# Two layers of causal attention on one core: row maxima taken two heads at a time, and a mask as products

## The chip, the core and the metric

The kernel runs on one core of a Trainium2 chip. Its time is the device time of one launch in microseconds (us); three runs before the change gave 3539.60, 3553.49 and 3558.32, a median of 3553.49. The engines are called as the profile calls them: PE is TensorE's matrix product, PEld its weight load, DVE is VectorE, ACT is ScalarE, POOL is GpSimd, and SP issues most transfers. Products are written to PSUM, which has eight banks of 512 float32 columns on 128 partitions.

## The reference, cut to what matters

```python
def _L0_ffn_ref(...):                       # layer 0, on xn = layernorm(x), as x below
    ...                                     # layernorm, Wqkv, rope
    scores = jnp.einsum('bqhd,bkhd->bhqk', q, k) / math.sqrt(hd)
    scores = jnp.where(causal, scores, -1000000000.0)
    probs = jax.nn.softmax(scores, axis=-1)
    attn = jnp.einsum('bhqk,bkhd->bqhd', probs, v).reshape(Bb, Tt, d) @ Wproj
    x = x + attn
    ...                                     # 8 experts, top 2, capacity 1024

def _L1_attn_ref(x, Wq, Wk, Wv, Wo):        # layer 1
    ...
    scores = (einsum(q_r, k_r) + einsum(q_i, k_i)) / jnp.sqrt(jnp.float32(hd))
    scores = jnp.where(causal[None, None], scores, -jnp.inf)
    probs = jax.nn.softmax(scores, axis=-1)
    ...                                     # times v_r, v_i, then Wo

x = L0_attn_x                               # 2 x 2048 x 256, 16 heads
x = x + _L0_attn_ref(xn) * silu(_L0_ffn_ref(xn))   # a linear attention beside the softmax attention
x = x + _L1_attn_ref(xn) * silu(_L1_ffn_ref(xn))   # xn is the layernorm of the new x
```

Both layers have a causal softmax attention over 2048 tokens, two batches and sixteen heads. A softmax needs the largest score of each row first.

## The kernel before

The work has three stages: layer 0's attention with a linear attention beside it, the experts, and layer 1's attention with its gates. Both attentions are made by `run_attention` (L513). Heads go in eight groups of four (two batches, four groups); the four heads of a group stand in four row groups of 32 partitions, so that four score products can run in the array side by side.

Each score is computed twice. **Pass A** (`pass_a`, L530) has queries on the partitions: for query tile `t` (128 queries) and key block `k` (up to 512 keys) the product of head `j` goes to a bank of its own (L535), and DVE takes the largest of each row. Off the diagonal it is one `tensor_reduce` (L546). On the diagonal (`k == t // 4`) the mask has to be added: `tensor_tensor_reduce` (L542) adds a table `causal` and takes the maximum; on the chip it is two instructions, the masked maximum and the read of its accumulator. When all tiles of a query block `c` (256 queries) are done, `subtract` brings the maxima to the other pass: in layer 0 they are added to the queries (L774 on), in layer 1 they become three bfloat16 rows that a product adds (`less_maximum`, L1485). **Pass B** (`pass_b`, L554) has keys on the partitions: the products of L561, on the diagonal a mask that is added by four bfloat16 products of 256 columns (`hide`, L500 to L504: `ident_h` times `mask_h`), then the exponential on ACT (L573). The weights times the values are products in column tiling (L803 in layer 0, L1516 in layer 1); in layer 1 POOL adds up the keys' weights (L1497 to L1502).

One step `u` of the loop handles one (t, k) of pass A for four heads and one key pair of pass B, one query block behind. Within it, two half units: heads `i` and `i + 1` do pass A while heads `i + 2` and `i + 3` do pass B, the four products alternating; then the pairs swap.

The order of the instructions isn't that of the loop. Every piece of work is a step with an engine, a price and the buffers that it reads and writes (`Plan.step`, L147). `Plan.run` (L273) searches, with a beam over random handicaps, for an order of all steps of a layer, and `places` (L181) gives each buffer the place of its kind that has been free for longest. PSUM banks are the kind `s`: eight places, each a tile of its own (`banks`, L446). Strand S is the main stream of PE, A the maxima, B the exponentials, V the sums of values; prep, sub, end, lin, mix and gate are other strands, and some of them may only hold a limited number of banks. The prices of the steps are the kernel's own (`t_row`, `t_dve`, `t_act`, L434 to L443).

Of the kernel before, what the change touches and what calls it, by code (L numbers as in the profile page):

```python
# [30 lines left out]
C_CAUSAL = C_ID + P  # L31
C_TRI = C_CAUSAL + 512
C_AFTER = C_TRI + P
# [8 lines left out]
def _constants():  # L42

    c = np.zeros((P, C_ALL), np.float32)
    r = np.arange(P)
    c[:, C_ID : C_ID + P] = np.eye(P)
    c[:, C_CAUSAL + 384 : C_CAUSAL + 512] = np.where(r[None] <= r[:, None], 0.0, FAR)
    c[:, C_TRI : C_TRI + P] = r[:, None] <= r[None]
    c[:, C_AFTER : C_AFTER + P] = np.where(r[:, None] > r[None], FAR, 0.0)
    c[:, C_BLOCK : C_BLOCK + P] = r[:, None] // 16 == r[None] // 16  # L50
    c[:, C_H8 : C_H8 + 8] = r[:, None] // 16 == np.arange(8)[None]
    c[:, C_H4 : C_H4 + 4] = r[:, None] // 32 == np.arange(4)[None]
    c[:, C_EREV : C_EREV + E] = E - np.arange(E)
    c[:, C_EIDX : C_EIDX + E] = np.arange(E)
    return c
# [15 lines left out]
class Buf:  # L71

    def __init__(self, kind):
        self.kind, self.n, self.uses, self.t = kind, None, 0, None

# [8 lines left out]
class State:  # L86


    def __init__(self, plan):
# [6 lines left out]
        self.guest = [None] * len(plan.bufs)  # L96
        self.since = {k: [0.0] * len(x) for k, x in plan.kinds.items()}
        self.free, self.groups = {}, [0.0] * 4
# [12 lines left out]
class Plan:  # L111
# [14 lines left out]


    GAP = 0.1
    MODE = 0.2
# [51 lines left out]
    def places(self, st, strand, s, t):  # L181

        take = []
        for b in s.bufs:
            if st.slot[b.n] is None:
                if b.kind == "s" and strand != "S" and st.held.get(strand, 0) >= self.QUOTA.get(strand, 1):
                    if sum(st.held.values()) >= self.GUESTS:
                        return None
                taken = [i for x, i in take if x.kind == b.kind]
                at, n = None, None  # L190
                for i, x in enumerate(st.since[b.kind]):
                    if x is not None and (at is None or x < at) and i not in taken:
                        at, n = x, i
# [6 lines left out]
    def advance(self, st, handicaps, until):  # L200
# [3 lines left out]
        while st.todo:  # L204
# [36 lines left out]
            for b, i in take:  # L241
                st.slot[b.n], st.since[b.kind][i] = i, None
                if b.kind == "s" and key[0] != "S":
                    st.guest[b.n] = key[0]
                    st.held[key[0]] = st.held.get(key[0], 0) + 1
# [18 lines left out]
            for b in s.bufs:  # L264
                st.left[b.n] -= 1
                st.until[b.n] = max(st.until[b.n], done)
                if st.left[b.n] == 0:
                    if st.guest[b.n]:
                        st.held[st.guest[b.n]] -= 1
                    st.since[b.kind][st.slot[b.n]] = st.until[b.n]  # L270
        return True

    def run(self):  # L273
# [36 lines left out]
        for s, take in order:  # L310
            for b, i in take:
                b.t = self.kinds[b.kind][i]()
            s.fn()
# [4 lines left out]
def kernel(ctx: ExitStack, tc: tile.TileContext, i: dict, out: bass.AP):  # L318
# [14 lines left out]
    ident = cst[:, C_ID : C_ID + P]  # L333
    causal = cst[:, C_CAUSAL : C_CAUSAL + 512]
    h4 = cst[:, C_H4 : C_H4 + 4]
# [39 lines left out]
    early = ctx.enter_context(ExitStack())  # L375
    w0 = early.enter_context(tc.tile_pool(name="w0", bufs=1))
    prelude = ctx.enter_context(ExitStack())
    pool = prelude.enter_context(tc.tile_pool(name="prelude", bufs=1))
# [20 lines left out]
    nc.sync.dma_start(wgate, rows(i["L0_ffn_Wgate"]))  # L399
    for n, c in enumerate((C_ID, C_AFTER)):  # L400
        m = bank().rearrange("p (q n) -> p q n", q=4)
        for q in range(4):
# [6 lines left out]
            )  # L409
        if n == 0:  # L410
            nc.vector.tensor_copy(ident_h, m)
        else:
            nc.vector.tensor_copy(mask_h, m[:, :, None].to_broadcast([P, 4, 2, P]))
    tp = bank("t")
# [30 lines left out]

    def banks(ps, names):  # L446
        return [lambda n=n: ps.tile([P, 512], F32, tag=n, name=n, bufs=1) for n in names]

# [50 lines left out]

    def hide(out, j):  # L500

        r = slice(32 * j, 32 * j + 32)
        for q in range(4):
            nc.tensor.matmul(out, ident_h[r, q], mask_h[r, q].rearrange("p n k -> p (n k)"), start=False, stop=q == 3)  # L504

# [6 lines left out]

    def run_attention(plan, make, prepare, subtract, sum_keys, finish, last_sum, before=None, others=(), between=False):  # L513

# [14 lines left out]

        def pass_a(g, t, k, j, w, mx, parts):  # L530

            s, r, out = Buf("s"), slice(32 * j, 32 * j + 32), (mx, t, k, j)

            def score():
                nc.tensor.matmul(  # L535
                    s.t[:, :w], g.qt.t[r, t * P : (t + 1) * P], g.kt.t[r, 512 * k : 512 * k + w], start=True, stop=True
                )

            def largest():
                to = mx.t[:, t % 2, j, k : k + 1]  # L540
                if k == t // 4:
                    nc.vector.tensor_tensor_reduce(  # L542
                        s.t[:, :w], s.t[:, :w], causal[:, 512 - w :], 1.0, -3e38, ALU.add, ALU.max, to
                    )
                else:
                    nc.vector.tensor_reduce(to, s.t[:, :w], AX.X, ALU.max)  # L546

            keys = range(4 * k, 4 * k + -(-w // P))
            step = S("S", "PE", t_row(w), score, r=[(g.qt, t), *((g.kt, n) for n in keys)], w=[s], on=j)
            S("A", "DVE", t_dve(w) + (0.19 if k == t // 4 else 0.0), largest, r=[s], w=[out])  # L550
            parts.append(out)
            return step

        def pass_b(g, c, p, j, pt):  # L554
# [11 lines left out]
            def rest():  # L566
                if before:
                    S("S", "PE", 0.25 * t_row(w), before(g, c, j, s, w, not diagonal), r=[s, g.mh[c]], w=[s], on=j)
                if diagonal:
                    S("S", "PE", T_HIDE, lambda: hide(s.t[:, : 2 * P], j), r=[s], w=[s], on=j)  # L570

# [9 lines left out]
        for u in range(at + last_sum + 1):  # L581
# [11 lines left out]
            for i in (0, 2):  # L593


                more = []
                for x in range(2):
                    if a:
                        plan.pace = pass_a(g, t, k, i + x, wa, mx, parts)
                        first = first or plan.pace  # L600
                    if b:
                        step, rest, weigh = pass_b(gb, cb, p, (i + 2 + x) % 4, pt)
                        first = first or step
                        more.append((rest, weigh))
                for rest, _ in more:
                    rest()
# [35 lines left out]
    with ExitStack() as sc:  # L642
# [13 lines left out]
        for vt in vts:  # L656
# [12 lines left out]
            dict(  # L669
                s=banks(ps, [f"s{n}" for n in range(8)]),  # L670
                qt=slots(wk, "qt", 2, [P, T]), kt=slots(wk, "kt", 2, [P, T]),
# [543 lines left out]
    for mpad in mpads1:  # L1215
        nc.gpsimd.memset(mpad, 0.0)
    lts = [w.tile([17, 512], F32, name=f"lt{n}") for n in range(2)]
    for lt in lts:
        nc.gpsimd.memset(lt, 1.0)

# [104 lines left out]
    with ExitStack() as sc:  # L1325
# [4 lines left out]
            dict(  # L1330
                s=banks(ps, [f"s{n}" for n in range(8)]),
                qt=slots(wk, "qt", 2, [P, T]), kt=slots(wk, "kt", 2, [P, T]), vt=slots(wk, "vt", 2, [P, NT, 4, 32]),
# [10 lines left out]
        S = plan.step  # L1343
        stats = norms(w, S)
        turned = {}

# [232 lines left out]
        def gate(b, c):  # L1579

            xt, pa, lt, ln = turned[b], Buf("s"), lts[c % 2], ("lt", c % 2)
            x_in_c = [(xt, c, t) for t in range(4 * c, 4 * c + 4)]
# [48 lines left out]
        others.sort(key=lambda x: x[0])  # L1631
        run_attention(plan, Group1, prepare, subtract, sum_keys, finish, SUM_LAG, less_maximum, others)
        with tc.manual_schedule():
# [29 lines left out]
```

## Time and profile before

| what | value |
|---|---|
| median of three runs | 3553.49 us |
| profiled execution | 3519.21 us, span 3517.3 us, mean granted clock 0.965 |
| PE, PEld busy | 3354.9 us (95%), 2382.7 us (68%) |
| DVE busy | 2160.5 us (61%) |
| ACT, POOL busy | 1680.8 us (48%), 1653.3 us (47%) |
| chain that ended last, by engine | PE 80%, POOL 11%, DVE 3%, waits for issue 2%, ACT 2% |
| layer 0, from 280 to 1130 us | PE 844.4, PEld 631.1, DVE 648.9, ACT 484.4, POOL 261.5 us |
| layer 1, from 2200 to 3400 us | PE 1179.8, PEld 834.3, DVE 820.1, ACT 620.1, POOL 937.9 us |

The page's groups name the line, the engine and operation, the written and read tiles, then the shapes (partitions x elements), the number of instructions, their busy time in us and the mean of one in ns, and last the idle time of the engine just before them with what ended most of it. "32*128" is the tiling of the array in rows and columns: 32*128 are the row-tiled score products, 128*32 the column-tiled products with the values, 128*128 the whole array. The ends of products are modelled by the profiler, so a product's record is longer than the time for which it fills the array; products in other row groups overlap it. Profiled execution and timed runs differ by 34 us, or 1%.

### The profile page before, as it was taken

What the parts mean: (1) busy time and instruction counts of PE and PEld (TensorE: products, weight loads), DVE (VectorE), ACT (ScalarE), POOL (GpSimd) and SP (SyncE); (2) the same over time, 40 slices, a digit from 0 to 9 for tenths busy, and PEclk for the clock granted to TensorE, in tenths of its full rate; (3) what the DMA queues carried; (4) which work ended last, traced back from release to release, by engine and by line L of the source; (5) the groups of instructions that cost most, each with busy time, mean ns of one, the idle gap of its engine ahead of it and who ended that gap; (6) DMA issues with size and microseconds to landing.
All of it is one profiled execution on the core that took longest, in us unless ns stands there. A gap on an engine that the chain in (4) does not pass through costs nothing.

```text
span 3517.3 us, 81236 instructions
## 1 busy us (share of the span) xinstructions
PE 3354.9 (95%) x33814; PEld 2382.7 (68%) x33814; DVE 2160.5 (61%) x5577; ACT 1680.8 (48%) x3341; POOL 1653.3 (47%) x2222
## 2 busy tenths in 40 slices
PE   6999999999999999599999699999999999999998
PEld 4777777777777776466666366666776667777775
DVE  5777777777777776411111366766666657667674
ACT  3565655555556555121111355545455555454544
POOL 4443222333233213300000357989777667877877
PEclk7999999999999999699999899999999999999998
DMA  5000000000000000222221211111000010000000
GB/s 180 2 2 2 8 8 8 19 29 16 8 11 5 14 8 24 84 68 74 78 72 46 89 53 43 33 43 31 21 8 27 31 39 14 22 13 22 11 19 28
DMA packets 88017, 115.38 MB, mean 33 GB/s; under 512 B 9043, under 2 KB 67103, under 8 KB 87650
## 3 DMA queue, kind: packets, MB, share of 16 engines
q1 hardware_dynamic: 81506, 96.32, 8.6%
q0 software_dynamic: 6144, 13.88, 1.3%
q8 instruction: 265, 4.34, 0.5%
q14 instruction: 102, 0.84, 0.1%
HBM read 75.33 MB, written 37.75 MB: 32 GB/s over the span
## 4 chain that ended last, share of the span: by engine, by line
PE 80%; POOL 11%; DVE 3%; issue 2%; ACT 2%; DMA 1%; SPq 0%; POOLq 0%; ACTq 0%; DVEq 0%
PE s L561 15%; PE s L535 14%; PE s L803 7%; PE s L1302 6%; PE s L1308 6%; PE s L1516 5%; PE s L1427 3%; PE s L504 3%; PE s L735 3%; POOL ps L1501 2%; PE s L1485 2%; POOL ps L1502 2%; POOL ps L1497 2%; PE s L359 2%; PE s L1522 2%
## 5 line engine op out<-in xcount | busy, mean ns | idle before, releaser
L573 ACT ACTIVATE pt<-s 128x512 f32<-128x512 f32 (+1 forms) x2304 | 1169.1, 576 | 709.2 <-PE s L561 246.0
L561 PE MATMUL s<-qt,kt 32*128 32x256 f32 (+1 forms) x9216 | 1297.6, 391 | 7.5 <-DVE un L810 3.3
L535 PE MATMUL s<-kt,qt 32*128 32x512 f32 (+3 forms) x5120 | 1269.8, 561 | 5.1 <-ACT pt L573 2.0
L546 DVE TENSOR_REDUCE mx<-s 128x1 f32<-128x512 f32 x1536 | 961.0, 682 | 193.2 <-PE s L535 111.4
L561 PEld LDWEIGHTS s<-qt,kt 32*128 32x128 f32 x9216 | 990.2, 187 | 61.3 <-ACT pt L573 9.8
L535 PEld LDWEIGHTS s<-kt,qt 32*128 32x128 f32 x5120 | 531.5, 187 | 165.0 <-issue 97.0
L542 DVE CUSTOM_DVE_ANT_0 s<-s,cst 128x128 f32<-128x128 f32 (+3 forms) x1024 | 481.3, 514 | 102.0 <-PE s L535 81.8
L1497 POOL TENSOR_TENSOR ps<-pt 128x1024 f32<-128x1024 f32 (+1 forms) x160 | 343.2, 2145 | 150.0 <-ACT pt L573 129.2
L742 POOL TENSOR_TENSOR ra<-raw,rope 128x128 f32<-128x128 f32 x128 | 58.6, 458 | 640.4 <-ACT raw L754 599.9
L1501 POOL TENSOR_TENSOR ps<-ps,pt 128x1024 f32<-128x1024 f32 x128 | 302.4, 2363 | 68.4 <-ACT pt L573 63.8
L1485 PE MATMUL s<-mh,ones_h 3*128 3x512 bf16 (+1 forms) x1152 | 321.9, 370 | 1.1 <-ACT mh L1478 1.1
L1362 POOL DMA_INDIRECT gx<-slots_out,back x64 | 62.8, 982 | 498.0 <-issue 496.4
L1311 DVE TENSOR_TENSOR ye<-s,b 128x256 f32<-128x256 f32 x64 | 27.2, 424 | 410.8 <-PE s L1308 410.8
L803 PE MATMUL s<-pt,vt 128*32 128x256 f32 (+1 forms) x4608 | 274.6, 377 | 0.6 <-ACT raw L754 0.5
L1502 POOL TENSOR_TENSOR ps<-ps,pt 128x1024 f32<-128x1024 f32 (+1 forms) x128 | 269.9, 2109 | 10.0
L1516 PE MATMUL s<-pt,vt 128*32 128x256 f32 (+1 forms) x4608 | 272.3, 375 | 0.7 <-ACT pt L573 0.4
L1303 ACT ACTIVATE hm<-s,b1c 128x512 f32<-128x512 f32 x128 | 87.8, 687 | 360.8 <-PE s L1302 360.8
L1302 PE MATMUL s<-xt,w 128*128 128x512 f32 x512 | 225.0, 598 | 7.1 <-DVE xt L1274 7.0
L1516 PEld LDWEIGHTS s<-pt,vt 128*32 128x32 f32 x4608 | 134.6, 111 | 137.9 <-ACT pt L573 19.7
L1308 PE MATMUL s<-w,hm 128*128 128x256 f32 x1024 | 223.6, 379 | 0.0
L803 PEld LDWEIGHTS s<-pt,vt 128*32 128x32 f32 x4608 | 135.3, 111 | 125.3 <-issue 21.9
L1308 PEld LDWEIGHTS s<-w,hm 128*128 128x128 f32 x1024 | 194.7, 190 | 33.1 <-issue 7.6
(257 smaller groups left out, 4240.6 us busy)
## 6 DMA issues: line engine op xcount, KB each, us to landing
w<-in_L_ffn_W_dram SPq DMA_DIRECT2D x16, 1024.0 KB, 5.6
gl<-g_dram SPq DMA_DIRECT2D x64, 256.0 KB, 2.7
slots_in<-zero SPq DMA_DIRECT2D x8, 1024.0 KB, 10.1
xe<-slots_in SPq DMA_DIRECT2D x16, 512.0 KB, 5.7
slots_out<-ye SPq DMA_DIRECT2D x16, 512.0 KB, 5.2
xr<-in_L_attn_x_dram SPq DMA_DIRECT2D x4, 1024.0 KB, 8.3
s_dram<-lo SPq DMA_DIRECT2D x16, 256.0 KB, 2.0
hn<-in_L_attn_x_dram SPq DMA_DIRECT2D x16, 256.0 KB, 2.7
```

The lines of the kernel that those rows point to most:

```text
L535: nc.tensor.matmul(s.t[:, :w], g.qt.t[r, t * P : (t + 1) * P], g.kt.t[r, 512 * k : 512 * k + w], start=True, stop=True)
L542: nc.vector.tensor_tensor_reduce(s.t[:, :w], s.t[:, :w], causal[:, 512 - w :], 1.0, -3e38, ALU.add, ALU.max, to)
L546: nc.vector.tensor_reduce(to, s.t[:, :w], AX.X, ALU.max)
L561: nc.tensor.matmul(s.t[:, at], g.kt.t[r, kj * P : (kj + 1) * P], g.qt.t[r, QC * c + q0 : QC * (c + 1)], start=n == 0, stop=n == 1 and not ...
L573: S("B", "ACT", t_act(w), lambda: nc.scalar.activation(pt.t[:, j, :w], s.t[:, :w], AF.Exp, scale=0.25), r=[s], w=[(pt, j)])
L803: nc.tensor.matmul(av.t[32 * j : 32 * j + 32, q0:QC], vts[G.vn][:, kj, j], pt.t[:, j, at], start=n == 0, stop=n == len(tiles) - 1,)
L1302: nc.tensor.matmul(ps, w1[:, k, f * P : (f + 1) * P], xt[:, k], start=k == 0, stop=k == 1)
L1308: nc.tensor.matmul(ps[:, :D], hm[:, f, s * P : (s + 1) * P], w2[:, f], start=f == 0, stop=f == FF // P - 1)
L1485: return lambda: nc.tensor.matmul(s.t[:, :w_], ones_h[r], G.mh[c].t[r, 512 - w_ :], start=False, stop=last)
L1497: nc.gpsimd.tensor_tensor(ps.t[:, :, q0:], pt.t[:, :, same], pt.t[:, :, odd], ALU.add)
L1501: nc.gpsimd.tensor_tensor(ps.t, ps.t, pt.t[:, :, even], ALU.add)
L1516: nc.tensor.matmul(av.t[32 * j : 32 * j + 32, q0:QC], G.vt.t[:, kj, j], pt.t[:, j, at], start=n == 0, stop=False)
```

## The change

Pass A makes its products of two neighbouring heads in two neighbouring banks. A buffer can now be a pair (`Buf("s", True)`): `places` looks for an even bank that is free together with the one after it, and the pair comes free as a whole. Off the diagonal one `tensor_reduce` over both banks gives both heads' maxima. On layer 0's diagonal the mask is added in the array, by four bfloat16 products of 128 columns for each head (`hide` with a new table `mask_q`), and the same pair maximum follows; on layer 1's diagonal the masked maximum of DVE stays, head by head. To make neighbours possible, PSUM in both layers is one tile of eight banks instead of eight tiles. The mask table of layer 1 moves from the constants into a tile of layer 1, and one of two `lt` buffers of the gates goes to make room.

```diff
@@ State, Plan.places
-        self.since = {k: [0.0] * len(x) for k, x in plan.kinds.items()}
+        self.since = {k: [0.0] * (plan.BANKS if k == "s" else len(x)) for k, x in plan.kinds.items()}
...
-                for i, x in enumerate(st.since[b.kind]):
+                for i in range(0, len(since), 2) if b.pair else range(len(since)):
+                    x = since[i]
+                    if b.pair and x is not None:
+                        x = max(x, since[i + 1]) if since[i + 1] is not None else None
@@ the tables, before layer 0
-    for n, c in enumerate((C_ID, C_AFTER)):
+    for n, c in enumerate((C_ID, C_AFTER, C_CAUSAL)):
...
+            nc.vector.tensor_copy(mask_q if n else ident_h, m)
@@ banks
-    def banks(ps, names):
-        return [lambda n=n: ps.tile([P, 512], F32, tag=n, name=n, bufs=1) for n in names]
+    def banks(ps):
+        all_ = ps.tile([P, Plan.BANKS, 512], F32, name="banks")
+        return lambda i, pair: all_[:, i : i + 2] if pair else all_[:, i]
@@ hide
-            nc.tensor.matmul(out, ident_h[r, q], mask_h[r, q].rearrange("p n k -> p (n k)"), start=False, stop=q == 3)
+            nc.tensor.matmul(out, ident_h[r, q], mask[r, q], start=False, stop=q == 3)
@@ run_attention
-        def pass_a(g, t, k, j, w, mx, parts):
-            s, r, out = Buf("s"), slice(32 * j, 32 * j + 32), (mx, t, k, j)
-            def score():
...
-            def largest():
...
+        def pass_a(g, t, k, i, w, mx, parts):
+            s, out, diagonal = Buf("s", True), (mx, t, k, i), k == t // 4
...
+            def products(x):
+                return S("S", "PE", t_row(w), lambda: score(x), r=[(g.qt, t), *((g.kt, n) for n in keys)], w=[(s, x)], on=i + x)
+            def rest():
+                for x in range(2) if diagonal and causal is None else ():
+                    S("S", "PE", T_HIDE / 2, lambda x=x: hide(s.t[:, x, w - P : w], i + x, mask_q), r=[(s, x)], w=[(s, x)], on=i + x)
+                if diagonal and causal is not None:
+                    for x in range(2):
+                        S("A", "DVE", t_dve(w) + 0.19, lambda x=x: nc.vector.tensor_tensor_reduce(
+                            s.t[:, x, :w], s.t[:, x, :w], causal[:, 512 - w :], 1.0, -3e38, ALU.add, ALU.max,
+                            mx.t[:, t % 2, i + x, k : k + 1],
+                        ), r=[(s, x)], w=[(*out, x)])
+                        parts.append((*out, x))
+                    return
+                S("A", "DVE", t_dve(2 * w), lambda: nc.vector.tensor_reduce(
+                    mx.t[:, t % 2, i : i + 2, k], s.t[:, :, :w], AX.X, ALU.max
+                ), r=[(s, 0), (s, 1)], w=[out])
+                parts.append(out)
...
+                if a:
+                    products, after_a = pass_a(g, t, k, i, wa, mx, parts)
                 for x in range(2):
                     if a:
-                        plan.pace = pass_a(g, t, k, i + x, wa, mx, parts)
+                        plan.pace = products(x)
                         first = first or plan.pace
...
+                if a:
+                    after_a()
                 for rest, _ in more:
                     rest()
@@ layer 1
-    lts = [w.tile([17, 512], F32, name=f"lt{n}") for n in range(2)]
+    lt = w.tile([17, 512], F32, name="lt")
...
+        causal = w.tile([P, 512], F32, name="causal")
+        nc.gpsimd.memset(causal[:, : 3 * P], 0.0)
+        nc.gpsimd.tensor_copy(causal[:, 3 * P :], cst[:, C_CAUSAL : C_CAUSAL + P])
...
-        run_attention(plan, Group1, prepare, subtract, sum_keys, finish, SUM_LAG, less_maximum, others)
+        run_attention(plan, Group1, prepare, subtract, sum_keys, finish, SUM_LAG, less_maximum, others, causal=causal)
```

## The prediction

> **What bounds the kernel now.** I read the page's busy table first, then the costliest groups, then the waits, then single stretches of the timeline.
>
> ```profile
> span 3517.3 us, 81236 instructions
> ...
> PE 3354.9 (95%) x33814; PEld 2382.7 (68%) x33814; DVE 2160.5 (61%) x5577; ACT 1680.8 (48%) x3341; POOL 1653.3 (47%) x2222
> ...
> L561 PE MATMUL s<-qt,kt 32*128 32x256 f32 (+1 forms) x9216 | 1297.6, 391 | 7.5 <-DVE un L810 3.3
> L535 PE MATMUL s<-kt,qt 32*128 32x512 f32 (+3 forms) x5120 | 1269.8, 561 | 5.1 <-ACT pt L573 2.0
> L546 DVE TENSOR_REDUCE mx<-s 128x1 f32<-128x512 f32 x1536 | 961.0, 682 | 193.2 <-PE s L535 111.4
> ...
> L542 DVE CUSTOM_DVE_ANT_0 s<-s,cst 128x128 f32<-128x128 f32 (+3 forms) x1024 | 481.3, 514 | 102.0 <-PE s L535 81.8
> ```
>
> TensorE is busy 95% and its score products show almost no idle time before them; DVE, whose maxima the change shortens, has 39% to spare and waits for PE. So PE's in-order queue sets the end. But a busy PE isn't a full PE. The next lines are the timeline of PE in layer 0.
>
> ```profile
> 951.18 0.61 PE L504 MATMUL s<-mask_h,ident_h 32*128 32x256 bf16 x8
> ...
> 951.73 1.93 PE L803 MATMUL s<-pt,vt 128*32 128x256 f32 x32
> 953.59 0.69 PE L535 MATMUL s<-kt,qt 32*128 32x512 f32 x1
> 953.60 0.48 PE L561 MATMUL s<-qt,kt 32*128 32x256 f32 x1
> ```
>
> Eight mask products, four for each of two heads, take 0.61 us together: the heads stand in different row groups and run side by side, each head's products 0.109 us apart (0.42 ns a column). A float32 product is two records, so 0.84 ns a column and record. With these rates I added up the columns of all records in stretches of row-tiled products. Layer 0 (80 to 1350 us): 285 stretches last 622 us, and the columns would fill four row groups for 464 us (some records are missing, so a little more). Layer 1 (2100 to 3450 us): 700 us for 514. About 340 us are thus lost inside "busy" PE: row groups of unequal length, and products that wait for a bank. In 60 us of these 340 the waiting weight load starts within 0.09 us of DVE's semaphore (29 and 31 us by layer), in 38 us of ACT's. A change of tiling mode leaves PE empty for 0.09 to 0.10 us (median of all changes).
>
> ```profile
> L504 PEld LDWEIGHTS <-ident_h x2048: 89/93/148, 42.8 to 3501.4; 32*128 32x128 bf16 x187
> L504 PE MATMUL s<-mask_h,ident_h x2048: 264/267/417, 42.9 to 3501.7; 32*128 32x256 bf16 x187
> ...
> 703.45 3.13 DVE L546 TENSOR_REDUCE mx<-s 128x1 f32<-128x512 f32 x5
> ...
> 1000.14 0.33 DVE L542 CUSTOM_DVE_ANT_0 s<-s,cst 128x128 f32<-128x128 f32 x1
> ...
> 1000.38 0.33 DVE L542 CUSTOM_DVE_ANT_0 s<-s,cst 128x128 f32<-128x128 f32 x1
> ```
>
> Records of 0.68 us overlap: five maxima in a row take 3.13, one each (3.13 - 0.68) / 4 = 0.61 us. The masked maximum with its accumulator read takes 0.25 us at 128 columns; its forms last 308, 445, 583 and 720 ns, so each 128 columns add 0.137 us: 0.25, 0.39, 0.52, 0.66.
>
> **The change part by part.** The profiled execution took 3519.2 us (span 3517.3), 34 us under the median of the runs, 3553.5; I make the sum against 3519.2 and move it to the median.
>
> Maxima of a pair. 768 pairs off the diagonal (both layers) and 256 on layer 0's. One 1024-column maximum: 0.61 + 512 x 1.07 ns = 1.16 us against 1.22, saving 0.06, 46 us of DVE in all (ends: nothing, if each bank pays its own start; 0.13 a pair, 100 us, if all of the fixed 0.134 us of the 682 ns record goes). On layer 0's diagonal, 64 pairs of each width: 0.33 + 0.61 + 0.88 + 1.16 = 2.98 us against two heads' 3.64, saving 42 us. DVE loses some 65 us in layer 0 and 23 in layer 1 of 2160. It is not the bound, so only the PE time that it holds up counts: at most the 60 us. Layer 0 sheds most, layer 1 keeps its masked maxima (L542). I take half, -30 us; ends 0 and -60.
>
> Mask of layer 0 as products. 512 head-tiles x 4 = 2048 products of 128 columns with as many weight loads. Columns: 0.0535 us each, 27.4 us over four row groups. In the built order of both programs I took, for each stretch of row products, the sum of the longest group: layer 0's array time goes from 1190.8 to 1211.3 us, +20.5, since the shorter heads are partly levelled; layer 1's +0.8. No row shows a 128-column bfloat16 product behind its own load. Bounds: 0.054 us (columns alone) and 0.095 (the 93 ns load record alone, if loads followed each other without overlap). In the lines above, loads of 93 ns don't stretch the 0.109 us pitch, so they run under the product before them, and where a second group starts its product follows its load by 0.016 us; I take 0.057. [...] by the trace 22. I take the trace, since its groups run side by side. Part of it lies under the row groups that stretch anyway: in half a unit, two heads do pass A while two do pass B (512 columns, 0.86 us); a masked A of 128 columns (0.21 + 0.23) or 256 (0.43 + 0.23) still ends first. Its cover is that imbalance; without it the full 22. I take 18; ends 0 and 36 (by the load).
>
> Order. The planner puts both layers in a new order. Changes of tiling mode: 671 to 722 in layer 0, 635 to 691 in layer 1, 107 x 0.096 = +10 us; some replace a wait for a bank, so +8 (ends 0 and 11). Layer 1's longer groups +1.
>
> One PSUM tile. Waits that PE must take as extra instructions fall from 416 to 263, 51 ns each in the trace, 8 us in a queue that mostly runs ahead: -4. ACT's rise from 648 to 972, DVE's from 545 to 754; most repeat what the PE product already waited for. ACT idles half of the time; 324 x 0.05 = 16 us of it, no cost unless a bank's release is late by them.
>
> Small edits. At the start DVE makes four more copies and a cast on the chain to the first norms (0.15 x 4 + 0.69 = 1.3 us), against a constant table 40% smaller in a load of 3.6 us: +1. Layer 1's mask table is filled by POOL, idle through the expert stage, and its single lt has its next writer behind the PE products that read it, nine units apart: 0; if that cover were gone, one gate's 2 us. No DMA is moved past another in SP's or POOL's queue; SP's issues stay 269.
>
> Sum: -30 + 18 + 8 + 1 - 4 + 1 = -6: a profile near 3513, a median near 3547.
>
> **The rivals.** (1) Main case: relief and masks nearly cancel, 3522 to 3572. (2) Clearly faster: DVE's releases were what kept PE from filling its rows, the full 60 us come back and the masks lie in the shadow of unequal groups: -60 + 0 + 8 + 1 - 4 + 1 = -54, 3500. For it: layer 0's row stretches of several units lose 2 us each, and DVE's semaphore ends a third of that; products that reuse a bank within 1.5 us of PE work fall in the new order (243 to 105 in layer 0, among passes A and B). Against: DVE holds 60 of 340 us only, and ends of queues move, they rarely vanish: ACT or PE's own groups come next, and POOL, 80% busy in layer 1, ends the last 70 us by its key sums. (3) Slower, by the pair's banks: two neighbouring banks are held until one 1.16 us maximum ends, where the first bank used to be free after 0.61, and the mask keeps them 0.23 us more. If the relief is used up by this and one pair in 30 (43 of 1280) holds PE 0.55 us longer: 0 + 18 + 8 + 1 - 4 + 1 + 24 = +48, 3601. It decides as soon as the row stretches' loss grows past today's 340 us. For it: 107 more mode changes say the planner found more gaps in its rows. (4) The change doing nothing is out: the built order has 1024 fewer masked-maximum instructions and 2048 more bfloat16 products.
>
> **How the numbers follow.** Main case 0.48, clearly faster 0.27, slower 0.25. A difference of about 0.5% (18 us) is what a measurement of this kernel can tell from no change. Of the main case 0.32 lies within it, 0.15 faster and 0.01 slower. So faster 0.42, same 0.32, slower 0.26. The likeliest: 3547. Range 3495 to 3598: down to the faster case, whose ends are DVE's 60 us, and up to the slower case; beyond lie about a tenth on each side. The main case's own range is 3522 to 3572.
>
> **What would show it.** After the change: 2048 more mask products in layer 0, their loads near 93 ns and two heads' eight in about 0.38 us; one pair maximum per 1.16 us; DVE near 2070 us busy; layer 0's row stretches filled to more than 75% if the relief came, less if pairs wait; PE's busy share still 94 to 96%. Wrong: row stretches of layer 1, where almost nothing is added, longer than before (the pair's banks); mask products 0.1 us apart (the loads); or a gain over 60 us, which would mean that DVE sets more of PE's time than its semaphores show.

## The result, and the profile after

| | median | runs | mean granted clock of the runs |
|---|---|---|---|
| before | 3552.84 us | 20, 3535.41 to 3562.15 | 0.963 (43 other runs) |
| after | 3535.22 us | 20, 3528.76 to 3540.93 | 0.971 |

The changed kernel takes 0.9956 of the time before, with an interval of 0.9945 to 0.9966: 17.6 us less by the medians. That is 0.44% faster, an amount between 0.34 and 0.55%. The time forecast was 3547, and the measured one lies inside its range, 12 us below it.

The profiled execution of after took 3536.29 us (span 3534.5), as long as its timed runs. That of before, 3519.2, was quicker than every timed run of its kernel. So profile against profile goes 17 us the wrong way, and stage times of the two must not be subtracted. What can be compared are counts, durations of single instructions and shares. The page of after:

```profile
span 3534.5 us, 84196 instructions
...
PE 3360.1 (95%) x35870; PEld 2348.1 (66%) x35870; DVE 2072.5 (59%) x4046; ACT 1682.1 (48%) x3343; POOL 1662.4 (47%) x2223
...
L567 DVE TENSOR_REDUCE mx<-banks 128x2 f32<-128x1024 f32 (+3 forms) x1024 | 1120.6, 1121 | 370.7 <-PE banks L581 147.0
L581 PE MATMUL banks<-qt,kt 32*128 32x256 f32 (+1 forms) x9216 | 1260.0, 388 | 9.3 <-ACT pt L593 5.0
L548 PE MATMUL banks<-kt,qt 32*128 32x512 f32 (+3 forms) x5120 | 1244.5, 561 | 13.2 <-DVE mx L567 7.5
...
L561 DVE CUSTOM_DVE_ANT_0 banks<-banks,causal 128x384 f32<-128x384 f32 (+3 forms) x512 | 242.2, 512 | 63.5 <-PE banks L548 55.0
```

L548 is the old L535 (products of pass A), L581 the old L561 (pass B), L567 the maximum of a pair, L561 layer 1's masked maximum. PE has 2056 product records more, of which 2048 are the masks, and is busy 95% as before. DVE is at 2072 us where some 2070 was forecast. It now stands idle longer in front of its maxima: 370.7 + 63.5 = 434 us, against 193.2 + 102.0 = 295 before (L546 and L542 on the page before). What DVE saved became idle time of DVE. The price of single pieces comes from the groups by form, from the view of the tile `mask_q`, and from the timelines of PE and DVE:

```profile
L567 DVE TENSOR_REDUCE mx<-banks 128x2 f32<-128x1024 f32 x832 | 990.2, 1221 | 275.4 <-PE banks L548 135.1 <-PE banks L581 89.2 <-PE banks L514 27.9
L514 PE MATMUL banks<-mask_q,ident_h x2048: 211/214/309, 32.1 to 1415.8; 32*128 32x128 bf16 x187
...
561.79 0.35 PE L514 MATMUL banks<-mask_q,ident_h 32*128 32x128 bf16 x6
...
563.24 0.35 PE L514 MATMUL banks<-mask_q,ident_h 32*128 32x128 bf16 x6
563.38 0.37 PE L581 MATMUL banks<-qt,kt 32*128 32x256 f32 x1
563.42 0.23 PE L514 MATMUL banks<-mask_q,ident_h 32*128 32x128 bf16 x2
...
698.88 2.36 DVE L567 TENSOR_REDUCE mx<-banks 128x2 f32<-128x1024 f32 x2
```

Two pair maxima in a row take 2.36 us with records of 1.22, so one each 2.36 - 1.22 = 1.14 us; 1.16 was forecast, against 2 x 0.61 for two heads before. Six mask products of two heads take 0.35 us. Two row groups of three each at the forecast pitch would take 2 x 0.057 + 0.214 = 0.33. All eight masks of two heads, as in the last three lines of PE, start within 0.19 us and last 0.40 us in all (the median of 235 such groups). At 0.056 us from start to start, one row group alone would need 0.39 us to start eight, so the two heads' masks run side by side, as forecast.

### The profile page after: what moved, and what is told of

Its sections match the earlier page's. It is cut to its first block, busy times and chain, and to the rows that moved or that the text cites. A ratio compares the mean times of both kernels' runs of the same rounds, so it can differ in the third digit from the quotient of the medians.

```text
span 3534.5 us, 84196 instructions
## 1 busy us (share of the span) xinstructions
PE 3360.1 (95%) x35870; PEld 2348.1 (66%) x35870; DVE 2072.5 (59%) x4046; ACT 1682.1 (48%) x3343; POOL 1662.4 (47%) x2223
## 4 chain that ended last, share of the span: by engine, by line
PE 80%; POOL 9%; DVE 4%; issue 3%; ACT 2%; another core or an unknown queue 1%; DMA 1%; POOLq 0%; SPq 0%; DVEq 0%; ACTq 0%
PE banks L548 15%; PE banks L581 13%; PE banks L827 7%; PE s L1325 6%; PE s L1331 6%; PE banks L1542 5%; PE banks L514 4%; PE banks L1453 3%; PE banks L759 3%; POOL ps L1527 2%; PE banks L1511 2%; DVE mx L567 2%; POOL ps L1528 2%; POOL ps L1523 2%; PE banks L366 2%
## 5 line engine op out<-in xcount | busy, mean ns | idle before, releaser
L593 ACT ACTIVATE pt<-banks 128x512 f32<-128x512 f32 (+1 forms) x2304 | 1167.3, 575 | 765.1 <-PE banks L581 215.9
L567 DVE TENSOR_REDUCE mx<-banks 128x2 f32<-128x1024 f32 (+3 forms) x1024 | 1120.6, 1121 | 370.7 <-PE banks L581 147.0
L581 PE MATMUL banks<-qt,kt 32*128 32x256 f32 (+1 forms) x9216 | 1260.0, 388 | 9.3 <-ACT pt L593 5.0
L548 PE MATMUL banks<-kt,qt 32*128 32x512 f32 (+3 forms) x5120 | 1244.5, 561 | 13.2 <-DVE mx L567 7.5
L581 PEld LDWEIGHTS banks<-qt,kt 32*128 32x128 f32 x9216 | 940.0, 186 | 53.7 <-ACT pt L593 12.9
L548 PEld LDWEIGHTS banks<-kt,qt 32*128 32x128 f32 x5120 | 487.3, 185 | 213.2 <-issue 116.4
L1511 PE MATMUL banks<-mh,ones_h 3*128 3x512 bf16 (+1 forms) x1152 | 298.7, 369 | 0.9 <-ACT mh L1504 0.9
L827 PE MATMUL banks<-pt,vt 128*32 128x256 f32 (+1 forms) x4608 | 276.3, 378 | 7.6 <-DVE mx L567 4.2
L561 DVE CUSTOM_DVE_ANT_0 banks<-banks,causal 128x384 f32<-128x384 f32 (+3 forms) x512 | 242.2, 512 | 63.5 <-PE banks L548 55.0
L1542 PE MATMUL banks<-pt,vt 128*32 128x256 f32 (+1 forms) x4608 | 270.8, 373 | 0.0
L1542 PEld LDWEIGHTS banks<-pt,vt 128*32 128x32 f32 x4608 | 134.2, 110 | 136.3 <-ACT pt L593 38.4
L827 PEld LDWEIGHTS banks<-pt,vt 128*32 128x32 f32 x4608 | 135.9, 111 | 127.7 <-issue 25.6
```

Of the source, the lines that this page charges most:

```text
L548: nc.tensor.matmul(s.t[:, x, :w], g.qt.t[r, t * P : (t + 1) * P], g.kt.t[r, 512 * k : 512 * k + w], start=True, stop=not (diagonal and cau ...
L567: S("A", "DVE", t_dve(2 * w), lambda: nc.vector.tensor_reduce(mx.t[:, t % 2, i : i + 2, k], s.t[:, :, :w], AX.X, ALU.max), r=[(s, 0), (s, ...
L581: nc.tensor.matmul(s.t[:, at], g.kt.t[r, kj * P : (kj + 1) * P], g.qt.t[r, QC * c + q0 : QC * (c + 1)], start=n == 0, stop=n == 1 and not ...
L593: S("B", "ACT", t_act(w), lambda: nc.scalar.activation(pt.t[:, j, :w], s.t[:, :w], AF.Exp, scale=0.25), r=[s], w=[(pt, j)])
L827: nc.tensor.matmul(av.t[32 * j : 32 * j + 32, q0:QC], vts[G.vn][:, kj, j], pt.t[:, j, at], start=n == 0, stop=n == len(tiles) - 1,)
L1511: return lambda: nc.tensor.matmul(s.t[:, :w_], ones_h[r], G.mh[c].t[r, 512 - w_ :], start=False, stop=last)
```

## The experiments

All ratios are to runs of the kernel before on the same chip, with 95% intervals. The theory to begin with was that of the prediction: DVE's relief pays for the masks and a little more. The rival that grew out of the runs: the order that the planner draws is what moves the time.

**Each layer, and the one tile.** `layer0_only` has the change in layer 0 and a copy of the old `run_attention` for layer 1.

```diff
+    def run_attention1(...):    # the function before: a bank a head, no products as masks
-        run_attention(plan, Group1, ...)
+        run_attention1(plan, Group1, ...)
```

> The change in layer 0 alone: pairs of banks, one PSUM tile and the mask as products there; layer 1 keeps single banks, eight tiles and its order of before. The sum of the prediction, taken by layer, gives layer 0 +2 us (DVE relief -20, masks +18, order +5, start +1, waits -2) and layer 1 -8 (relief -10, order +4, waits -2): so 3553 to 3557 here, and the 16 us of the whole change should be missing. If instead DVE's relief is worth what DVE saves (layer 0 has three quarters of it), the time is 3535 to 3542 and layer 1 adds next to nothing.

It took 3548.46 us, ratio 0.9996 [0.9978, 1.0013]: layer 0's part of the change nets nothing that shows, within 6 us either way. By subtraction the 0.4% would stand in layer 1, where only the pairs of banks, the one tile of PSUM and the order differ. This isn't shown directly: the profiles of after and `layer0_only` are 10 us apart, and 7 of these arise before the experts, where both do the same (the experts' first product starts at 1510.2 and 1517.2 us).

```diff
-        return [lambda n=n: ps.tile([P, 512], F32, tag=n, name=n, bufs=1) for n in names]
+        all_ = ps.tile([P, 8, 512], F32, name="banks")
+        return [lambda n=n: all_[:, n] for n in range(8)]
```

> The kernel before with its eight PSUM tiles made one tile of eight banks; same order of instructions, only the waits differ. Theory (the relief of DVE makes the gain): -4 us at most, 3549 to 3553. Rival (PE's queue gains from needing fewer waits): most of the 16 us, 3536 to 3542.

`one_tile` took 3555.40 us, 1.0005 [0.9986, 1.0024]: the waits that go and come with one PSUM tile cost nothing that shows.

**The masks doubled, and issued in turn.** `dup_mask` makes every mask product of layer 0's pass A twice, in after's order.

```diff
-        for q in range(4):
-            nc.tensor.matmul(out, ident_h[r, q], mask[r, q], start=False, stop=q == 3)
+        times = 2 if mask is mask_q else 1
+        for n in range(times):
+            for q in range(4):
+                nc.tensor.matmul(out, ident_h[r, q], mask[r, q], start=False, stop=q == 3 and n == times - 1)
```

> The changed kernel, same order, with each of layer 0's mask products of pass A made twice (the mask is added twice, which leaves the weights as they are): 2048 more products of 128 columns. Array time by the longest row groups goes from 1211 to 1240 us. If masks cost what the sum says (18 of 22 us for the first 2048), +25 us on the changed kernel: about 3560. If they lie in the shadow of waits and unequal groups, +0 to +8: 3536 to 3544. If loads set their pace (0.095 us), +45: 3580.

It took 3612.07 us, 1.0174 [1.0146, 1.0202]: 77 us on top of after, where all three expectations were between 0 and 45. The longest row groups grow only by some 29 us of array time (1211 to 1240). I read the row-tiled stretches of both traces. Stretches in which pass A has 256 keys and pass B runs beside it lose some 0.45 us each in after, 1.0 with the second set; with 512 keys of A beside an unmasked B it is some 0.35 in both. So the loss is where the masks are, and more than their columns. The timeline of PE in `dup_mask` shows why a second set costs more than a first:

```profile
601.46 0.21 PE L516 MATMUL banks<-mask_q,ident_h 32*128 32x128 bf16 x1
601.52 0.33 PE L516 MATMUL banks<-mask_q,ident_h 32*128 32x128 bf16 x3
601.69 0.23 PE L516 MATMUL banks<-mask_q,ident_h 32*128 32x128 bf16 x2
601.74 0.40 PE L516 MATMUL banks<-mask_q,ident_h 32*128 32x128 bf16 x7
601.99 0.33 PE L516 MATMUL banks<-mask_q,ident_h 32*128 32x128 bf16 x3
```

Four products start alone, at the pitch of one row group; the second head's first starts 0.23 us after the first head's first, beside its fifth. The sixteen masks of two heads so last 0.85 us (the median of 222 such groups), 0.45 more than the eight of after, where eight products of two heads side by side would add 4 x 0.056 = 0.22. The 0.45 us of 256 such groups are 115 us, of which 77 show in the end. A set of four for each head runs side by side, a set of eight does so in part only. `dup_mask` is therefore no measure of what the first set costs.

My next theory was PE's queue: the second head's masks stand behind the first head's in the program, and so the two row groups don't run side by side. In `mask_interleaved` both heads' products are issued in turn, in the same order of steps otherwise.

```diff
-                    S("S", "PE", T_HIDE / 2, lambda x=x: hide(s.t[:, x, w - P : w], i + x, mask_q), ...)
+                    S("S", "PE", T_HIDE / 2, lambda x=x: hide_both(x), ...)
+                def hide_both(x):
+                    if x == 0:
+                        return
+                    for q in range(4):
+                        for y in range(2):
+                            h = slice(32 * (i + y), 32 * (i + y) + 32)
+                            nc.tensor.matmul(s.t[:, y, w - P : w], ident_h[h, q], mask_q[h, q], start=False, stop=q == 3)
```

> After, in the same order, but the mask products of a pair of heads are issued alternately (quarter 0 of the first head, quarter 0 of the second, and so on) instead of four of one head and then four of the other. Numbers of products and weight loads are unchanged. Theory 'queue': the masks cost some 38 us (after against pairs_dve_mask) although their columns add only 20 us of array time, because PE takes its instructions in order and the second head's products stand behind the first head's, which wait for their own row group. Then issuing them alternately, so that two row groups run side by side, gives a good part of it back: 15 to 30 us faster than after, ratio to before 0.987 to 0.991, and two heads' eight masks in about 0.3 us. Rival 'columns': the row groups are simply filled, or the masks wait for their own head's score product whatever the issue order: within 8 us of after, ratio 0.993 to 0.998. Rival 'loads': alternating row groups makes each load change its group and costs more: over 10 us slower than after.

It took 3536.93 us, 0.9947 [0.9929, 0.9965], the same as after. The timeline of PE in `mask_interleaved` shows that the products do run as meant:

```profile
565.69 0.34 PE L563 MATMUL banks<-mask_q,ident_h 32*128 32x128 bf16 x6
565.83 0.37 PE L589 MATMUL banks<-qt,kt 32*128 32x256 f32 x1
565.87 0.22 PE L563 MATMUL banks<-mask_q,ident_h 32*128 32x128 bf16 x2
```

The eight masks of two heads start within 0.18 us (565.69 to 565.87) and end at 566.09, 0.40 us in all. But the lines of after above, where the program has four of one head and then four of the other, show the same 0.19 and 0.40 us. So the queue theory falls by after's own trace: the masks already ran side by side there, and the other order of issue changed nothing that PE did. The prediction called the queue in-order; between two row groups it was not so for sets of four products (eight starts within 0.19 us).

**The maxima, one bank at a time.** `split_max` is after with two reductions of one bank in place of each pair's one.

```diff
-                S("A", "DVE", t_dve(2 * w), lambda: nc.vector.tensor_reduce(
-                    mx.t[:, t % 2, i : i + 2, k], s.t[:, :, :w], AX.X, ALU.max
-                ), r=[(s, 0), (s, 1)], w=[out])
+                def each():
+                    for x in range(2):
+                        nc.vector.tensor_reduce(mx.t[:, t % 2, i + x, k : k + 1], s.t[:, x, :w], AX.X, ALU.max)
+                S("A", "DVE", t_dve(2 * w), each, r=[(s, 0), (s, 1)], w=[out])
```

> The changed kernel, same order and prices, with each pair maximum made as two maxima of one bank each: DVE works some 50 to 70 us more, all else equal. Theory (DVE's releases hold up PE, half of what DVE saves is felt): +20 to +30 us on the changed kernel, 3556 to 3566, so that the gain is gone. Rival (DVE has slack, the gain comes from the order or the waits): within 5 us of the changed kernel, 3532 to 3542.

It took 3540.61 us, 0.9967 [0.9953, 0.998]. The page of `split_max` says how much work DVE got back, 2132.8 us busy where after has 2072.5:

```profile
PE 3374.1 (95%) x35870; PEld 2374.5 (67%) x35870; DVE 2132.8 (60%) x5070; ACT 1681.1 (48%) x3343; POOL 1664.3 (47%) x2223
```

60 us more of DVE's time, of the 88 that the change had saved, move the end by 4 us by the ratios and 5 by the medians, and the intervals of the two kernels overlap. The joined maximum is at most a small part of what makes after faster than before. (The other 28 us, which DVE saves on layer 0's diagonal, were not given back by themselves.)

**Masks without pairs, pairs without masks.** `mask_only` keeps a bank for each head and adds layer 0's mask as products; `pairs_dve_mask` has the pairs and leaves the masked maxima on DVE in both layers, with the mask table in the constants again.

```diff
# mask_only, against before
+            masked = causal is None and k == t // 4
...
-                if k == t // 4:
+                if k == t // 4 and not masked:
...
+            def rest():
+                if masked:
+                    S("S", "PE", T_HIDE / 2, lambda: hide(s.t[:, w - P : w], j, mask_q), r=[s], w=[s], on=j)
...
# pairs_dve_mask, against after
...
-        run_attention(plan, Group0, ..., others=others, between=True)
+        run_attention(plan, Group0, ..., others=others, between=True, causal=causal)
```

> Layer 0's mask of pass A as bfloat16 products, on single banks: a plain maximum of one bank follows. Layer 1 keeps its order of before (its mask table stands in a tile of layer 1 and there is one lt buffer). Array time of layer 0 by longest groups 1191 to 1217 us, DVE sheds some 0.05 us on each of 512 maxima and their reads. Theory (masks cost PE time, the pairs bring the relief): +10 to +20 us, 3563 to 3573. Rival (taking the mask from DVE is what helps): 3535 to 3545.

`mask_only` took 3550.03 us, 0.9959 [0.9946, 0.9973], in a series in which before itself took 3564.48. By the ratio this is 15 us faster than before, in the range of the rival, where the theory had expected a loss. But its layer 0 has an order of its own, so the runs on the order, further on, have to be read with it.

> Pairs of banks and one PSUM tile in both layers, with the masked maxima left on DVE head by head in both; layer 1 in the order of the changed kernel, layer 0 in one of its own with 737 changes of tiling mode against 722. No mask products. By the prediction's sum without the masks' 18 us and with less of the relief (-15 instead of -30): about -6, 3547. If the products are what makes pairs pay on the diagonal, no gain or a loss: 3550 to 3565. If pairs alone make the gain and the masks only cost: 3520 to 3530.

`pairs_dve_mask` took 3507.32 us, 0.9848 [0.9822, 0.9874], the fastest kernel of the study, and faster than all three expectations. Its order has the most changes of tiling mode of all (737 and 691 in the two layers; before 671 and 635), which by my way of pricing an order should have made it slow.

`pairs_dve_split` is `pairs_dve_mask` with the edit of `split_max`, in the same order.

> pairs_dve_mask (pairs and one PSUM tile in both layers, all masked maxima on DVE), in the same order, but each pair's maximum off the diagonal is two maxima of one bank each. DVE gets 0.06 us back per pair, 46 us in all. Theory 'order': what made pairs_dve_mask 1.5% faster than before is the order in which the plan puts pairs (fewer lulls of PE, a higher granted clock, row groups better levelled), not DVE's shorter work: within 8 us of pairs_dve_mask, ratio to before 0.983 to 0.988, clock near 0.971. Rival 'DVE': the joined maximum frees banks earlier and PE gains by it: 20 to 45 us slower than pairs_dve_mask, ratio 0.991 to 0.998.

It took 3518.43 us, 0.9900 [0.9877, 0.9924]. This lies between what the two theories expected: without the masks the joined maximum is worth some 11 us by the medians and 18 by the ratios, for 46 us of DVE's time (2103.8 us busy on the page of `pairs_dve_mask`, 2149.4 on that of `pairs_dve_split`). The greater part of the 54 us that `pairs_dve_mask` gains on before in its one order is not DVE's.

**Other draws of the order.** The planner's random search has a seed. Each of these kernels does the same work as its parent, with the steps in another order: `after_seed` and `before_seed` and `pairs_dve_seed` with seed 1, `before_seed2` with seed 2.

```diff
-        draw = random.Random(0)
+        draw = random.Random(1)    # before_seed2: 2
```

> The changed kernel with another seed of the planner's random handicaps: the same work in another order (716 and 673 changes of tiling mode). If the gain lies in the work, within 6 us of the changed kernel, 3531 to 3543. If it is the luck of an order, anything from 3520 to 3560.

> The kernel before with that other seed (655 and 636 changes). If the gain lies in the work, 3547 to 3559, as before. If orders differ by luck as much as the change moved the time, outside of it by 10 us or more either way.

> pairs_dve_mask with the other seed of the planner's random search in both layers. Theory 'pairs help': pairs without mask products are worth about 1.5% in most orders: ratio to before 0.980 to 0.988. Rival 'luck of an order': the 1.5% belongs to one order, since another seed moved before by 0.8%: ratio 0.990 to 1.000.

> Before with a third seed of the planner's search. It tells how far orders of one and the same work lie apart: seed 1 gave a ratio of 0.992 to the seed of before. Theory 'before drew a slow order': again 0.990 to 0.995, with a granted clock near 0.970; then after's gain is what another draw gives. Rival 'before is typical': 0.998 to 1.003, with a clock near 0.963; then seed 1 was the exception and the change's gain more than a draw.

| kernel | ratio, seed 0 | seed 1 | seed 2 | mean |
|---|---|---|---|---|
| before | 1 | 0.9918 [0.9891, 0.9945] | 0.9950 [0.9937, 0.9963] | 0.9956 |
| after | 0.9956 [0.9945, 0.9966] | 0.9930 [0.9903, 0.9956] | | 0.9943 |
| pairs, masks on DVE | 0.9848 [0.9822, 0.9874] | 0.9903 [0.9879, 0.9927] | | 0.9876 |

The medians were 3537.30 us (`after_seed`), 3532.15 (`before_seed`), 3519.05 (`pairs_dve_seed`) and 3536.05 (`before_seed2`). By what was expected of them, `after_seed` alone speaks for the work; the other three speak for the luck of an order. Two other orders of the kernel before, with nothing changed, are 0.5% and 0.8% faster than the one it had. That is as much as the whole change brings. Over the draws, after stands 0.0013 below before, 5 us, which so few draws can't tell from zero. Pairs without mask products stand 0.0080 below before, some 28 us, and 0.0067 below after, some 24 us. Of the 28 us the joined maximum accounts for 11 to 18, by `pairs_dve_split`; where the rest comes from is not shown. Both of their draws are faster than all five of the others, but two and three draws are few: the nearest two, 0.9903 and 0.9918, have intervals that overlap, and the runs of before in the two series behind these ratios differ by 11 us (3564.48 and 3553.40). `mask_only`, at 0.9959, is where the mean of before is (0.9956): with single banks its one draw shows no cost of the masks.

The masks can also be read in layer 0 alone. The first product of the experts ends that stage. These are the lines of that product, in order, from after, `after_seed`, `pairs_dve_mask`, `pairs_dve_seed`, before and `one_tile` (the two times after the durations are the first and the last start):

```profile
L1325 PE MATMUL s<-xt,w x512: 592/592/1222, 1510.2 to 1962.3; 128*128 128x512 f32 x171
```

```profile
L1325 PE MATMUL s<-xt,w x512: 592/592/1222, 1506.7 to 1958.7; 128*128 128x512 f32 x171
```

```profile
L1326 PE MATMUL s<-xt,w x512: 592/592/1222, 1481.9 to 1933.5; 128*128 128x512 f32 x171
```

```profile
L1326 PE MATMUL s<-xt,w x512: 592/592/1221, 1483.3 to 1935.5; 128*128 128x512 f32 x171
```

```profile
L1302 PE MATMUL s<-xt,w x512: 592/592/1222, 1493.7 to 1945.4; 128*128 128x512 f32 x171
```

```profile
L1303 PE MATMUL s<-xt,w x512: 592/592/1222, 1516.3 to 1967.9; 128*128 128x512 f32 x171
```

With pairs and the masks as products the stage ends at 1510 and 1507 us, with pairs and the masks on DVE at 1482 and 1483: 28 and 23 us apart, in both draws. One profile each would not carry this, since before and `one_tile` have the same order and are 23 us apart. But three more profiles with after's layer 0 (`mask_interleaved`, `split_max`, `layer0_only`) end the stage at 1507 to 1517 us, and `pairs_dve_split` at 1487, so all five of the one kind lie 20 us or more above all three of the other. The other two orders of before end it at 1474 and 1499, `mask_only` at 1512. So with pairs, masks as products cost layer 0 some 20 to 30 us beside masks on DVE. That pairs alone shorten layer 0 does not stand out from the orders of before.

**The clock.** What differs between the orders of before besides waits is the granted clock. The timed runs of before have a mean of 0.963 on one chip and 0.960 and 0.961 in two other series; `before_seed` has 0.970, `before_seed2` 0.968, after 0.971. Among 43 runs of before, one and the same program, 0.001 more of clock goes with 2.3 us less (correlation -0.73); in the two other series, 27 runs each, with 1.9 and 1.5. At these rates the 0.0083 between before and after are 13 to 19 us, most or all of the change's 17.6. One such place in before's trace, by windows (columns: window, its length, busy time of PE, PEld, DVE, ACT, POOL, the clock, then DMA), and PE's timeline in it:

```profile
700.00:720.00 20.00, 20.00 (x231) 15.22 (x227) 17.46 (x59) 11.83 (x25) 8.84 (x15) 1.00 0.10 34
720.00:738.00 18.00, 16.24 (x98) 13.96 (x99) 8.69 (x36) 7.50 (x17) 7.00 (x20) 0.62 0.06 22
738.00:760.00 22.00, 21.96 (x247) 15.58 (x246) 18.29 (x68) 13.16 (x27) 7.59 (x16) 1.00 0.06 20
```

```profile
722.20 1.06 PE L929 MATMUL s<-wgate,at 128*128 128x8 f32 x8
723.49 0.33 PE L763 MATMUL s<-cst,pad 128*128 128x128 f32 x1 [0.23 <-POOL pad L751]
725.30 0.90 PE L763 MATMUL s<-cst,pad 128*128 128x128 f32 x3 [1.49 <-POOL pad L751]
```

PE has eight products of eight columns, waits 0.23 us and then 1.49 us for POOL, and is "busy" 16.24 of the 18 us around it; the clock of these 18 us is 0.62 (1.00 until 724.3 us, then 0.50 from within the wait of 1.49 us to 738.0), which takes up to 18 x 0.38 = 6.8 us of full-speed work on top of the waits. Between 30 and 1450 us the stretches at a clock of 0.50 add up to 96 us in before's trace and 63 in after's, but 75 in that of the faster `pairs_dve_mask`. The longest wait in these 18 us is 1.49 us, and the clock fell within it. A longer one left the clock as it was: later in the same trace PE waits 2.24 us between products of 128 columns and more, and the clock stays at 1.00:

```profile
2199.73 0.44 PE L1547 MATMUL s<-cst,rw 128*128 128x128 f32 x2 [2.24 <-ACT rw L1553]
```

```profile
2190.00:2200.00 10.00, 7.76 (x77) 4.42 (x71) 8.71 (x10) 6.77 (x13) 9.84 (x4) 1.00 0.00 0
2200.00:2210.00 10.00, 10.00 (x124) 7.42 (x122) 9.04 (x22) 5.85 (x11) 8.84 (x13) 1.00 0.01 2
```

What sets the fall is not settled by these traces.

Two kernels with mask products in layer 0 and before's order in layer 1 fit in part only: `layer0_only` and `mask_only` both have a clock of 0.968, 0.005 and 0.0085 above before in their series. `layer0_only` gains 5 us by the medians and 1 by the ratio, less than the 11 that 2.3 us for each 0.001 would give; `mask_only` gains 15, about the 16 that the 1.9 of its series gives, so no cost of its masks is left to see.

That the clock carries the difference is argued from these correlations and not shown: it may be that a run that waits longer has a lower clock for that reason, and no kernel filled the lulls of before's order with other products. It also leaves a rest: the profiled execution of before had a clock of 0.965, and was some 30 us quicker than its timed runs at that clock; `one_tile`, in the same order and profiled at the same 0.965, took 3551.68 us. Why is open.

## Why the prediction was right or wrong

That the total came near is luck. The sum said -6 us for one pair of orders, and gave the order itself no more than 0 to +11. Over the draws of the order the change is worth about -5, which so few draws can't tell from nothing; the measured -17.6 contains, beyond that, a slow draw of before. Within the sum, DVE's relief was too large for after's order and the masks too small. What made up for both, the order drawn and whatever pairs bring besides DVE's time, was not in the sum.

- **DVE's relief, -30 us: the step that failed.** The durations under it were right (1.14 us a pair against 1.16, 88 us less for DVE in all, DVE at 2072 us against 2070). The step from DVE's time to PE's was wrong: DVE's semaphore standing last before 60 us of late weight loads was taken as half convertible, which is 30 us for 88 of DVE, or a third. Giving DVE 60 us back moved the end by 4 to 5 us in after's order, less than a tenth; the forecast's low end, 0, was nearer. In the order of `pairs_dve_mask`, without mask products, 46 us given back moved it by 11 to 18, a quarter to two fifths, as forecast. So the rate is no property of the maxima alone. Why it differs between the two is open.
- **The filling of layer 0's rows was no test.** They filled to 78%, above the 75% that I had named as the sign of relief. But the faster `pairs_dve_mask` fills 462 of 618 us, 75%, as before did. The share rose since mask products are themselves filling: the columns went from 464 to 481.5 us in stretches of 622 and 616. A share that the change itself feeds says nothing of its gain.
- **Masks, +18 us: right in kind, too small.** With pairs, draws of the order say 24 us, layer 0's stage 23 and 28. These are already net of the 42 us of DVE's time that the masks as products save on the diagonal. For `pairs_dve_mask` against after the sum had +18 and -15, so +3. The pitch held: within one row group consecutive mask products start 0.055 to 0.056 us apart in after, with load records of 93 ns under them, so columns (128 at 0.42 ns, 0.054 us) and not loads set the pace in these runs of four. What seems mis-sized is the part in shadow: I let 4 of 22 us (20.5 us of columns, at a pitch of 0.057 instead of 0.0535 us) vanish under unequal row groups, and 23 to 28 us leave no room for that. Which products stretch by it was not isolated, and with single banks (`mask_only`) the one order measured shows no such cost.
- **Order, +8 us: the wrong measure.** I priced the order by its changes of tiling mode, 107 x 0.096 us. The kernel with the most changes is the fastest, and before's three orders (671 and 635, 655 and 636, 685 and 648 changes in layers 0 and 1) stand at 1, 0.9918 and 0.9950, not by their number. The draws of one kernel lie 9 to 29 us apart, and I gave the term ends of 0 and 11. This is the largest fault of the working, since it decides between "same" and "faster" by itself.
- **One PSUM tile, -4 us, and layer 1's longer groups, +1:** nothing that shows (1.0005 with the tile alone).
- **Rival of a clear gain:** its sign and size came true in a kernel that is not the change, since `pairs_dve_mask` takes 3507 us; but a third or less of its 54 us on before is DVE's. **Rival of a loss by the pair's banks:** did not occur. Layer 1's row stretches, its stated sign, last 688 us in after and 688 in the same window of before (2110 to 3440 us).

## What to carry to other kernels

Where a search or a scheduler fixes the order, measure both kernels under several seeds before an edit is credited or blamed: here the same work in three orders spreads by 0.8%, twice the effect of the edit. Split a mixed change and keep the part that pays: pairs with their masked maxima left on an engine with 40% to spare gain 1.0 to 1.5% on the order that before had (0.8% on the mean of its orders, in few draws), and moving the masks to the engine that is the bound gives most of that back. How much of the time saved on an engine off the bound is felt can't be read from late waits alone: here it was less than a tenth in one order and a quarter to two fifths in another. Try it by giving the work back, which is one edit.

## What the runs showed of the hardware

- In before's trace, after eight products of eight columns and a wait of 0.23 us, PE's clock went from 1.00 to 0.50 within a wait of 1.49 us and stayed there for about 14 us (0.62 over 18 us), though PE counts as 90% busy in these 18 us. A wait of 2.24 us between products of 128 columns and more, in the same trace, left it at 1.00. The mean clock goes with the order of instructions: 0.960 to 0.963 for before in every series, 0.968 to 0.970 for the other orders of the same work.
- A weight load of 93 ns hides beside products of 128 columns in its own row group: in sets of four they still start 0.055 to 0.056 us apart (after).
- Products of two row groups ran side by side although the program has four of one and then four of the other (eight in 0.40 us); with eight and eight, the second group started beside the first one's fifth (sixteen in 0.85 us). Issuing fours in turn changed nothing (3536.93 against 3535.22 us).
- A maximum over two banks costs DVE 1.14 us where two maxima of one bank cost 2 x 0.61, by single pieces; by DVE's busy time over all widths the joined instruction saves 0.06 us (60.3 us for 1024 pairs in `split_max`).
